# Lags that shrink one at a time over the last 24 groups of a graph-network kernel

## The chip, the cores and the metric

The kernel runs on one core of a Trainium2 chip. The metric is the device time of one execution in microseconds (us), lower is better. A core has five engines with a queue of instructions each, worked off in order: TensorE (PE in the profile; its weight loads are PEld), VectorE (DVE), ScalarE (ACT), GpSimd (POOL) and SyncE (SP). They wait for each other on semaphores. DMAs are issued from the queues of SyncE, ScalarE and GpSimd.

## The reference

There are 12,500 nodes with 64 features each, `x`, and 200,000 edges with a source, a target (sorted), 64 features and a distance. Cut to what matters:

```python
nodes = node_state[edges].reshape(num_edges, -1)          # source and target rows, 128 wide
gates = ssp(edge_state @ We1 + be1) @ We2 + be2           # ssp(x) = softplus(x) - log 2
soft_cutoff = 1.0 - sigmoid(5.0 * (edges_distance - 3.5))
gates = gates * soft_cutoff
h = ssp(nodes @ Wn1 + bn1) @ Wn2 + bn2
messages = h * gates
message_sum = zeros_like(node_state).at[edges[:, 1]].add(messages)
new_state = node_state + (ssp(message_sum @ Ws1 + bs1) @ Ws2 + bs2)
x = layernorm(x + new_state)
```

So every edge passes two small networks of two layers (one on its own features, one on its two nodes), the products are summed by target node, and then every node passes one more network of two layers and a normalization.

## The kernel before

**Groups.** Edges are worked in 391 groups of 512, numbered 0 to 390. A group is 4 lanes of 128 edges. Since targets are sorted, the targets of half a group lie in a window of 42 nodes; window positions are read from a table at run time.

**Stages of a group g**, with the line that the profile shows for each:
- `gather` (L230): GpSimd fetches the source rows, one indirect DMA per lane, into one of 18 buffers `xg`, 14 groups ahead. For 40 lanes out of the whole, SyncE and ScalarE fetch the 128 rows one by one instead (`fetch`, L244 loads row numbers into registers, L250 issues the DMAs): eight rows a step from ScalarE's queue, in three places of its step, six from SyncE's.
- `load` (L270, L278): SyncE fetches edge features `eT` and 42 rows per half group of a table with the target's share of layer 1, into `wns`, five steps ahead.
- `onehot` (L285): VectorE writes the edges' places in the window, 0 or 1, beside the source rows.
- `transposes` (L299, L296 for rows fetched one by one): TensorE, four, into a PSUM tile `tx` (two buffers); `xcopy` (L304): ScalarE copies it to SBUF.
- layer 1: `layer1_bias` (L309), `layer1_edge` (L314), `layer1_node` (L320): TensorE, into a PSUM tile `z` of two banks (two buffers).
- `exps` (L331), `logs` (L334): ScalarE; `softplus` (L339): VectorE, which makes `s`.
- layer 2: `layer2_edge` (L345 the biases, L348 the edges' half), `layer2_node` (L354): TensorE, into `gh` (two buffers).
- `hcut` (L363) and `message` (L367): VectorE.
- `scatter` (L371): TensorE sums messages by place in the window; `window` (L388): VectorE adds this to `sums` at the window's position.

**Node blocks.** Nodes are finished in blocks of 512 as soon as their sums are complete: `hidden` (L407) and `clamp` (L422, L423), logarithms (L426, L427), centring (L417, L418), `ssp` (L430), second layer (L435, L438) and `add` (L442), square, variance, root, scale (L446 to L464) and the store (L467). The parts of a block are dealt out to later steps. Parts with a TensorE half are called early in a step.

**Order.** All is written out by hand in program order (`manual_schedule`); each engine keeps that order, and waits are derived from the tiles. A program loop runs over steps i. In the main loop step i does, on TensorE: layer 1 bias of group i+1 (this instruction also takes, in one place, the waits for the loads and the copy of i+1 and for gather and one-hot of group i+3), layer 2 of edges of group i-1, layer 1 of i+1, sums of i-3 (into a free part of the `z` tile of i+1), transposes of i+3, layer 2 of nodes of i-1. So three lags exist: transposes are 2 groups ahead of layer 1, layer 2 is 2 groups behind it (`second`), sums are 4 behind it (`third`).

**Catch-up.** The last steps shrink these lags. `ends` is the step 10 before the last group (380). The lag of sums falls by one after step 378 and once more after 385, that of layer 2 after 383; from step 380 on, a second form of the step is used (the `else` branch): transposes and copy of the next group, layer 1, exponential and logarithm, layer 2 of group i, softplus of i+1, and then the sums, into a `tx` tile, with their window. Then a tail handles group 390, the last sums, and the last node block.

Of the kernel before, what the change touches and what calls it, by code (L numbers as in the profile page):

```python
# [59 lines left out]
HE = 256  # L60
GE = 2 * HE
W = 42
DW = D + W
PIECES = 3
NB = 512
K = 4
AHEAD = 14
LOADS = 5
SPREADS = 5
CATCH_UP = 10  # L70
PREPARE = 5
# [50 lines left out]
def gnn_resnorm_kernel(ctx: ExitStack, tc: tile.TileContext, a: dict, out: bass.AP, E: int):  # L122
    nc = tc.nc
# [64 lines left out]
    def note(key, ins):  # L188
        made.setdefault(key, []).append(ins)
        return ins  # L190
# [18 lines left out]
    def arrived(g, k):  # L209
        n = by_rows[g, k]  # L210
        queue = slots[n][0]
        n -= firsts[queue]
        return landed[queue][n % LANDED], 16 * P * (n // LANDED + 1)
# [77 lines left out]

    def transposes(g):
        tx = tx_tile()[:DW].rearrange("f (k e) -> f k e", k=K)
        for k in range(K):
            if (g, k) in by_rows:
                note(("rows read", by_rows[g, k]), nc.tensor.transpose(tx[:, k, :], xrs[g, k][:, :DW], ident)  # L296
                     .wait_op(*arrived(g, k), "sem-ge"))
            else:
                nc.tensor.transpose(tx[:, k, :], xgs[g][:, k, :DW], ident)  # L299
        xTs[g] = tx  # L300

    def xcopy(g):
        xT = work.tile([DW, K, P], F32, name="xT", bufs=3)
        note(("xcopy", g), nc.scalar.copy(xT, xTs[g]))  # L304
        xTs[g] = xT.rearrange("f (t h) e -> f h t e", h=2)
# [35 lines left out]

    def layer2_edge(g):
        gh = gh_tile()
        v = gh.rearrange("p (i t h d) -> p i t h d", i=2, t=2, h=2)
        nc.tensor.matmul(gh, ones3[:, :P], row3.rearrange("q i k d -> q (i k d)"), start=True, stop=False,  # L345
                         skip_group_check=True)
        for t in range(2):
            nc.tensor.matmul(v[:, 0, t], ss[g][:, 0, t, :], we2, start=False, stop=False, skip_group_check=True)  # L348
        ghs[g] = gh.rearrange("p (i k d) -> p i k d", i=2, k=K)

# [127 lines left out]
    with tc.manual_schedule():  # L478
# [130 lines left out]
        with tc.tile_pool(name="finish", bufs=1) as finish:  # L609
            blocks = list(zip(node_blocks(N), block_steps(N, NG)))  # L610
            last = NG - 1
            ends = last - CATCH_UP
            second, third, ahead = {}, {}, {}

            def lagging(i, lag, steps):

                lag -= sum(i > step for step in steps)
                return [g for g in range(i - lag, i - lag + 1 + (i in steps)) if g >= 0]

            for i in range(-3, NG):  # L620
                second[i] = lagging(i, 1, (ends + 3,))
                third[i] = lagging(i, 3, (ends - 2, ends + 5))
                ahead[i] = [i + 3] if i < ends else [i + 2] if i == ends + 1 else [i + 1] if i > ends + 2 else []
            parts, begun, complete, rest = {}, None, 0, []
# [9 lines left out]
            for i in range(-3, last - 1):  # L634
# [5 lines left out]
                if i >= 0:  # L640
                    at(gather, i + AHEAD, i < BEHIND)
                if i < ends:
                    needs = [("xcopy", i + 1), ("load", i + 1)]
                    needs += [(name, g) for g in ahead[i] for name in ("gather", "onehot")]
                    if i >= -1:
                        layer1_bias(i + 1, *needs)
                    for g in second[i]:
                        layer2_edge(g)
                    if i >= -1:
# [25 lines left out]
                else:  # L675
                    for g in ahead[i]:
                        transposes(g)
                        xcopy(g)
                    layer1_bias(i + 1)
                    layer1_edge(i + 1)  # L680
                    for part in early:
                        part.tensor(zs[i + 1][:, 1, HE:])
                    layer1_node(i + 1)
                    exps(i + 1)
                    logs(i + 1)
                    for g in second[i]:
                        layer2(g)
                        hcut(g)
                        message(g)
                    softplus(i + 1)  # L690
                    for g in third[i]:
                        scatter(g, tx_tile()[:, : 2 * W])
                        window(g)
                    for part in early:
# [19 lines left out]

            begun.pop(2).others()
            transposes(last)
            xcopy(last)
            layer1_bias(last)
            layer1_edge(last)
            layer1_node(last)  # L720
# [4 lines left out]
            square()  # L725
            for g in range(last - 2, last + 1):
                window_bases(g)
            layer2(last - 1)
            scatter(last - 2, tx_tile()[:, : 2 * W])
            softplus(last, edge)  # L730
            hcut(last - 1)
            message(last - 1)
            layer2_edge(last)
            scatter(last - 1, tx_tile()[:, : 2 * W])
            softplus(last, node)
            window(last - 2)
            variance()
            root()
            layer2_node(last)
            window(last - 1)  # L740
            hcut(last)
            message(last)
            scatter(last, tx_tile()[:, : 2 * W])
            window(last)
            hidden, clamp = begun.pop(0)
# [153 lines left out]
```

## Time and profile before

| | |
|---|---|
| time, median of 3 runs | 1969.16 us (1963.82 to 1975.15) |
| profiled execution: time, span | 1968.45 us, 1966.5 us |
| PE busy, mean granted clock | 1750.5 us (89%), 0.97 |
| GpSimd's last gather is issued | 1919.68 us |
| first exponential of group 366, of group 380, of group 390 | 1820.64, 1887.75, 1946.17 us |
| first layer of the last node block starts | 1952.89 us |

The profile is one execution. Busy time counts what an engine worked; matmuls are pipelined, so their rows overlap, and the distance between starts tells more than their length. In a timeline a row is start, length, engine, line, operation and shapes, the number of instructions merged, and in brackets the idle time ahead and what ended it. The granted clock is TensorE's clock as a share of full speed. Program line numbers are those of the kernel before.

### The profile page before, as it was taken

The numbers are of one execution on the slowest core, as the hardware profiler recorded it, in microseconds if no ns is written. First come the engines' busy times: TensorE is split into PE (matmuls) and PEld (weight loads), VectorE is DVE, ScalarE is ACT, GpSimd is POOL, SyncE is SP. The second block draws the span as 40 slices with busy tenths as digits, with TensorE's granted clock in tenths as the row PEclk, the third lists the DMA queues.
The fourth block names the chain that finished last, engine by engine and source line by source line (L and its number), as shares of the span: only waits on it lengthen the run. The fifth ranks groups of instructions, "written<-read, shape, count | busy, mean of one in ns | idle before, by whom it ended". The sixth has DMA issues, their size and how long they took to land.

```text
span 1966.5 us, 46634 instructions
## 1 busy us (share of the span) xinstructions
PE 1750.5 (89%) x11373; PEld 1491.4 (76%) x11373; DVE 1077.2 (55%) x2774; ACT 922.5 (47%) x1318; POOL 1445.0 (73%) x1527
## 2 busy tenths in 40 slices
PE   5899999999998988889889988998989989998896
PEld 4777877877777777777777777777777777777775
DVE  4455555555555555555555555555555555555654
ACT  1344545555454444445444444444544454444443
POOL 6777777777777777777777777777777777777770
PEclk9999999999999999999999999999999999999997
DMA  8422222222222222222222222222222222222220
GB/s 242 128 70 65 70 64 72 65 72 65 73 67 73 65 73 67 67 66 69 65 69 66 67 70 67 69 67 70 68 70 73 64 74 68 70 72 71 69 61 13
DMA packets 149240, 143.45 MB, mean 73 GB/s; under 512 B 50073, under 2 KB 96621, under 8 KB 148964
## 3 DMA queue, kind: packets, MB, share of 16 engines
q1 hardware_dynamic: 92972, 88.12, 15.6%
q0 software_dynamic: 48736, 50.00, 11.3%
q10 hardware_dynamic: 7256, 2.27, 0.6%
q8 instruction: 97, 1.59, 0.3%
q14 instruction: 179, 1.47, 0.3%
HBM read 130.59 MB, written 9.63 MB: 71 GB/s over the span
## 4 chain that ended last, share of the span: by engine, by line
PE 46%; ACTq 14%; DMA 10%; SPq 10%; issue 9%; ACT 5%; DVE 3%; POOL 3%; DVEq 0%; POOLq 0%
ACTq L250 11%; PE z L320 10%; PE gh L348 7%; PE gh L354 6%; PE z L314 5%; PE z L371 5%; DMA xg<-in_x,src_i 4%; PE tx L299 4%; DMA wns<-table 4%; SPq L250 4%; ACT u L331 3%; ACTq L244 3%; PE z L309 3%; POOL xg L230 3%; PE gh L345 2%
## 5 line engine op out<-in xcount | busy, mean ns | idle before, releaser
L230 POOL DMA_INDIRECT xg<-in_x,src_i x1523 | 1444.8, 949 | 475.3 <-issue 319.4
L331 ACT ACTIVATE u<-z 128x768 f32<-128x768 f32 x392 | 315.9, 806 | 624.4 <-PE z L371 316.7
L334 ACT ACTIVATE u<-u,one 128x768 f32<-128x768 f32 x392 | 366.0, 934 | 238.5 <-ACT u L331 236.7
L339 DVE SCALAR_TENSOR_TENSOR s<-u,z 128x768 f32<-128x768 f32 x392 | 372.6, 950 | 171.2 <-ACT u L334 154.6
L363 DVE TENSOR_TENSOR h<-gh,cut 128x256 f32<-128x256 f32 x391 | 165.2, 423 | 478.3 <-PE gh L354 472.0
L320 PE MATMUL z<-xT,wns 106*128 106x256 f32 x1564 | 423.9, 395 | 0.0
L354 PE MATMUL gh<-consts,s 128*128 128x64 f32 x3128 | 395.7, 270 | 0.0
L354 PEld LDWEIGHTS gh<-consts,s 128*128 128x128 f32 x3128 | 384.7, 194 | 0.0
L320 PEld LDWEIGHTS z<-xT,wns 106*128 106x128 f32 x1564 | 307.4, 198 | 45.8 <-ACT xT L304 0.7
L348 PEld LDWEIGHTS gh<-consts,s 128*128 128x128 f32 x1564 | 206.7, 192 | 122.8 <-issue 122.3
L348 PE MATMUL gh<-consts,s 128*128 128x128 f32 x1564 | 282.4, 304 | 0.0
L371 PEld LDWEIGHTS z<-xg,msg 128*128 128x128 f32 x1512 | 237.9, 199 | 22.9
L309 PE MATMUL z<-ones,be 3*128 3x256 bf16 x391 | 105.3, 269 | 167.8 <-DMA wns<-table 64.9
L299 PE MATMUL tx<-consts,xg 128*106 128x128 f32 x1524 | 240.8, 280 | 4.0 <-DVE xg L285 2.7
L388 DVE TENSOR_TENSOR sums<-sums,z 64x42 f32 x756 | 148.7, 197 | 171.4 <-ACT u L331 75.2
L314 PE MATMUL z<-eT,consts 128*128 128x256 f32 x782 | 242.4, 393 | 0.0
L304 ACT COPY xT<-tx 106x512 f32<-106x512 f32 x391 | 221.6, 567 | 15.5 <-PE tx L299 15.3
L371 PE MATMUL z<-xg,msg 128*128 128x84 f32 x1512 | 223.3, 271 | 0.0
L309 PEld LDWEIGHTS <-be 3*128 3x128 bf16 x391 | 35.4, 91 | 206.6 <-issue 102.9
L299 PEld LDWEIGHTS tx<-consts,xg 128*106 128x106 f32 x1524 | 181.8, 144 | 5.1 <-DVE xg L285 3.0
L367 DVE TENSOR_TENSOR msg<-gh,h 128x256 f32<-128x256 f32 x391 | 165.9, 424 | 13.4
L345 PE MATMUL gh<-row,ones 3*128 3x512 bf16 x391 | 145.9, 373 | 0.0
(103 smaller groups left out, 714.0 us busy)
## 6 DMA issues: line engine op xcount, KB each, us to landing
eT<-in_eT SPq DMA_DIRECT2D x195, 256.0 KB
xr<-in_x ACTq DMA_DIRECT2D x2944, 0.2 KB
xr<-in_x SPq DMA_DIRECT2D x2176, 0.2 KB
xg<-in_x,src_i POOLq DMA_INDIRECT x1523
wns<-table SPq DMA_DIRECT2D x782, 21.0 KB
table<-tb SPq DMA_DIRECT2D x14, 448.0 KB
sums<-in_xT SPq DMA_DIRECT2D x7, 455.0 KB
y<-in_x SPq DMA_DIRECT2D x24, 128.0 KB
```

Source lines behind the costliest of these rows:

```text
L230: note(("gather", g), nc.gpsimd.indirect_dma_start(out=xg[:, k, :D], out_offset=None, in_=x, in_offset=bass.IndirectOffsetOnAxis(ap=src_i[ ...
L250: ins = queues[queue].dma_start(row_tiles[n, "in"][r + j : r + j + 1, :D].bitcast(U8), x_bytes[:, bass.ds(row_at[queue][j], 4 * D)])
L299: nc.tensor.transpose(tx[:, k, :], xgs[g][:, k, :DW], ident)
L304: note(("xcopy", g), nc.scalar.copy(xT, xTs[g]))
L314: nc.tensor.matmul(zs[g][:, 0, :HE], we1.rearrange("a h d -> a (h d)"), eTs[g], start=False, stop=True, skip_group_check=True)
L320: nc.tensor.matmul(zn, wns[:, g % REST, h, :], xTs[g][:, h], start=True, stop=True, skip_group_check=True)
L331: nc.scalar.activation(us[g][:, part], z_of(g)[:, part], AF.Exp)
L334: nc.scalar.activation(us[g][:, part], us[g][:, part], AF.Ln, bias=one)
L339: nc.vector.scalar_tensor_tensor(ss[g].rearrange("p i t e -> p (i t e)")[:, part], us[g][:, part], BIG, z_of(g)[:, part], OP.min, OP.max)
L348: nc.tensor.matmul(v[:, 0, t], ss[g][:, 0, t, :], we2, start=False, stop=False, skip_group_check=True)
L354: nc.tensor.matmul(ghs[g][:, 1, 2 * t + h, :], ss[g][:, 1 + h, t, :], wn2, start=False, stop=h == 1 and t == 1, skip_group_check=True)
L371: ins = nc.tensor.matmul(sc, msgs[g][:, 2 * t : 2 * t + 2, :].rearrange("p h f -> p (h f)"), xgs[g][:, 2 * t : 2 * t + 2, D:DW], start=t = ...
```

## The change

The second form of the step gets another order and is used for 21 steps (368 to 388) in place of 9 (380 to 388). In it TensorE does transposes of group i+1, both biases, the sums (into the free part of the `z` tile, as in the main loop), layer 1 of i+1, and then all of layer 2 of its group. VectorE adds windows ahead of h and message, and softplus comes after them. Parts of node blocks go behind layer 2, into a `tx` tile. Transposes of this form wait at their first instruction for the loads, gather and one-hot of their group.

The lags shrink at one step each: transposes from 3 groups ahead to 1 in steps 366 and 367, which are main-loop steps that transpose nothing; layer 2 after step 374 (374 does two groups); sums after 376 and after 378. The biases of layer 2 are a function of their own, `layer2_bias`; in the main loop it is called where these biases stood before. The tail is put in the same order, with layer 2 of group 390 ahead of h and message of 389.

```diff
-CATCH_UP = 10
+CATCH_UP = (24, 16, 14, 12)
...
-    def transposes(g):
+    def transposes(g, *needs):
...
+            if k == 0:
+                behind(ins, *needs)
...
-    def layer2_edge(g):
+    def layer2_bias(g):
         gh = gh_tile()
-        v = gh.rearrange("p (i t h d) -> p i t h d", i=2, t=2, h=2)
         nc.tensor.matmul(gh, ones3[:, :P], row3.rearrange("q i k d -> q (i k d)"), start=True, stop=False,
                          skip_group_check=True)
+        ghs[g] = gh.rearrange("p (i k d) -> p i k d", i=2, k=K)
+
+    def layer2_edge(g):
+        v = ghs[g].rearrange("p i (t h) d -> p i t h d", t=2)
         for t in range(2):
             nc.tensor.matmul(v[:, 0, t], ss[g][:, 0, t, :], we2, start=False, stop=False, skip_group_check=True)
-        ghs[g] = gh.rearrange("p (i k d) -> p i k d", i=2, k=K)
...
-            ends = last - CATCH_UP
+            ends, *takes = (last - n for n in CATCH_UP)
...
-                second[i] = lagging(i, 1, (ends + 3,))
-                third[i] = lagging(i, 3, (ends - 2, ends + 5))
-                ahead[i] = [i + 3] if i < ends else [i + 2] if i == ends + 1 else [i + 1] if i > ends + 2 else []
+                second[i] = lagging(i, 1, takes[:1])
+                third[i] = lagging(i, 3, takes[1:])
+                ahead[i] = [i + 3] if i < ends else [i + 1] if i > ends + 1 else []
...
-                if i < ends:
+                if i < ends + 2:
...
                     for g in second[i]:
+                        layer2_bias(g)
                         layer2_edge(g)
...
                 else:
-                    for g in ahead[i]:
-                        transposes(g)
-                        xcopy(g)
+                    transposes(i + 1, ("load", i + 1), ("gather", i + 1), ("onehot", i + 1))
+                    xcopy(i + 1)
                     layer1_bias(i + 1)
+                    for g in second[i]:
+                        layer2_bias(g)
+                    for n, g in enumerate(third[i]):
+                        scatter(g, zs[i + 1][:, 1, HE + 2 * W * n : HE + 2 * W * (n + 1)])
                     layer1_edge(i + 1)
-                    for part in early:
-                        part.tensor(zs[i + 1][:, 1, HE:])
                     layer1_node(i + 1)
                     exps(i + 1)
                     logs(i + 1)
+                    for g in third[i]:
+                        window(g)
                     for g in second[i]:
                         layer2(g)
                         hcut(g)
                         message(g)
+                    for part in early:
+                        part.tensor(tx_tile())
                     softplus(i + 1)
-                    for g in third[i]:
-                        scatter(g, tx_tile()[:, : 2 * W])
-                        window(g)
                     for part in early:
                         part.others()
...
-            transposes(last)
+            transposes(last, ("load", last), ("gather", last), ("onehot", last))
             xcopy(last)
             layer1_bias(last)
+            layer2_bias(last - 1)
+            scatter(last - 2, zs[last][:, 1, HE : HE + 2 * W])
...
-            for g in range(last - 2, last + 1):
+            window(last - 2)
+            for g in range(last - 1, last + 1):
                 window_bases(g)
             layer2(last - 1)
-            scatter(last - 2, tx_tile()[:, : 2 * W])
+            layer2_bias(last)
             softplus(last, edge)
+            layer2_edge(last)
+            softplus(last, node)
+            layer2_node(last)
             hcut(last - 1)
             message(last - 1)
-            layer2_edge(last)
             scatter(last - 1, tx_tile()[:, : 2 * W])
-            softplus(last, node)
-            window(last - 2)
             variance()
             root()
-            layer2_node(last)
-            window(last - 1)
             hcut(last)
             message(last)
             scatter(last, tx_tile()[:, : 2 * W])
+            window(last - 1)
             window(last)
```

More of the change, by code (lines that the diff above doesn't have):

```diff
@@ L295, in transposes @@
             if (g, k) in by_rows:
-                note(("rows read", by_rows[g, k]), nc.tensor.transpose(tx[:, k, :], xrs[g, k][:, :DW], ident)
-                     .wait_op(*arrived(g, k), "sem-ge"))
-            else:
-                nc.tensor.transpose(tx[:, k, :], xgs[g][:, k, :DW], ident)
+                ins = nc.tensor.transpose(tx[:, k, :], xrs[g, k][:, :DW], ident)
+                note(("rows read", by_rows[g, k]), ins.wait_op(*arrived(g, k), "sem-ge"))
+            else:
+                ins = nc.tensor.transpose(tx[:, k, :], xgs[g][:, k, :DW], ident)
+            if k == 0:
+                behind(ins, *needs)
         xTs[g] = tx
```

## The prediction

> **What bounds the kernel now.** I read the page's busy shares and costliest groups, then GpSimd's own timeline, then the start of every exponential (line 331) as the clock of the steps, then TensorE's timeline in a step without waits and in the last steps, and last the busy time and granted clock in stretches of 3.4 us.
>
> ```profile
> PE 1750.5 (89%) x11373; PEld 1491.4 (76%) x11373; DVE 1077.2 (55%) x2774; ACT 922.5 (47%) x1318; POOL 1445.0 (73%) x1527
> ...
> L230 POOL DMA_INDIRECT xg<-in_x,src_i x1523 | 1444.8, 949 | 475.3 <-issue 319.4
> ```
>
> ```profile
> 1918.43 0.94 POOL L230 DMA_INDIRECT xg<-in_x,src_i  x1 [0.31 <-issue]
> 1919.68 0.95 POOL L230 DMA_INDIRECT xg<-in_x,src_i  x1 [0.30 <-issue]
> ```
>
> GpSimd looks 73% busy, but its gathers follow each other every 1.25 us (0.95 busy, 0.30 of issue) from the start to 1920.6: 4.99 us for a group of four gathers, 3.74 for one of three. That paces the main loop. A step without waits needs less of TensorE:
>
> ```profile
> 1884.87 0.28 PE L309 MATMUL z<-ones,be 3*128 3x256 bf16 x1
> 1884.99 0.37 PE L345 MATMUL gh<-row,ones 3*128 3x512 bf16 x1
> 1885.29 0.71 PE L348 MATMUL gh<-consts,s 128*128 128x128 f32 x4
> 1885.84 0.60 PE L314 MATMUL z<-eT,consts 128*128 128x256 f32 x2
> 1886.28 1.03 PE L320 MATMUL z<-xT,wns 106*128 106x256 f32 x4
> 1887.14 0.57 PE L371 MATMUL z<-xg,msg 128*128 128x84 f32 x4
> 1887.55 0.60 PE L299 MATMUL tx<-consts,xg 128*106 128x128 f32 x4
> 1887.98 1.00 PE L354 MATMUL gh<-consts,s 128*128 128x64 f32 x8
> 1888.92 0.28 PE L309 MATMUL z<-ones,be 3*128 3x256 bf16 x1
> ```
>
> From start to start that is 4.05 us: 0.12 first bias, 0.30 second bias, 0.55 layer 2 of edges, 0.44 layer 1 of edges, 0.86 layer 1 of nodes, 0.41 sums, 0.43 transposes, 0.94 layer 2 of nodes. Layer 1 of group i+1 waits, by its list of needs, for the gather of group i+3, so TensorE stays some two groups behind what it could do. The last gather is issued at 1919.68, yet group 390, the last, starts its exponential only at 1946.17 and the end is at 1966.5. The place to look at is this stretch:
>
> ```profile
> 1820.64 0.79 ACT L331 ACTIVATE u<-z 128x768 f32<-128x768 f32 x1
> ...
> 1920.49 0.94 DVE L339 SCALAR_TENSOR_TENSOR s<-u,z 128x768 f32<-128x768 f32 x1
> 1921.35 0.95 DVE L388 TENSOR_TENSOR sums<-sums,tx 64x42 f32 x4
> ...
> 1921.87 1.05 PE L299 MATMUL tx<-consts,xg 128*106 128x128 f32 x4 [1.31 <-issue]
> ...
> 1936.91 0.74 PE L438 MATMUL z<-consts,l_s 128*128 128x128 f32 x4 [2.01 <-DVE l_s L430]
> ...
> 1946.17 0.38 ACT L331 ACTIVATE u<-z 128x256 f32<-128x256 f32 x1 [2.39 <-PE z L320]
> ```
>
> The first line is the exponential of group 366, the last that of group 390: 125.5 us for 24 groups, 5.23 each. In its last ten steps the mean is 5.84. The lines between show two of the causes: transposes wait for a `tx` buffer that two sums hold until softplus and window are through, and the node block's second layer waits on TensorE for VectorE. And each such stall has an aftermath in the granted clock:
>
> ```profile
> 1863.90:1867.30 3.40, 1.61 (x10) 1.25 (x11) 2.93 (x9) 0.75 (x2) 2.49 (x4) 1.00 0.31 98
> 1867.30:1870.70 3.40, 3.40 (x15) 3.13 (x14) 0.56 (x2) 1.07 (x2) 2.57 (x3) 0.50 0.16 34
> 1918.50:1921.90 3.40, 2.09 (x20) 1.97 (x20) 2.04 (x6) 1.13 (x2) 1.82 (x2) 1.00 0.13 29
> 1921.90:1925.30 3.40, 3.40 (x10) 2.47 (x11) 1.03 (x4) 0.58 (x1) 0.00 (x0) 0.50 0.02 5
> ```
>
> The columns are the stretch, its length, busy time of PE, PEld, DVE, ACT, POOL, the granted clock, and DMA. A stretch in which TensorE was busy 1.6 to 2.3 of 3.4 us is followed by one at clock 0.50. Between 1820 and 1946 that is so at 1836.6, 1867.3, 1921.9 and (6.8 us long) 1939.0: five stretches, each worth up to 1.7 us, 8.5 together.
>
> **The change, part by part.** Up to the step of layer 1 of group 366 both kernels issue the same; the bias matmul split off layer 2 of edges stays at its place there. So I count from 1820.64 to the first exponential of group 390, and then the rest.
>
> *Two steps without transposes (groups 367, 368).* Transposes to 368 are already made. ScalarE bounds these: before, its round is 4.32 (exponential 0.81, half the row fetches 0.65, logarithm 0.94, four row DMAs 1.39, copy 0.57, overlaps off). 3.95 as before for 367, then 4.32 less a copy, 3.75: 1828.3. ScalarE's row fetches end with step 367 (736 pieces, two a step); SyncE's earlier. So none is dropped by the longer catch-up.
>
> *The turn (369).* The copy of 369 comes behind the logarithm of 368 (2.40 after its exponential) and behind the last four row DMAs (1.39), takes 0.57, and layer 1 of nodes to the exponential is 1.07 to 1.17 in this trace: 1833.8. Before had 1833.23; TensorE idles some 1.5 us once.
>
> *The new step.* Order: transposes, biases, sums, layer 1, layer 2. From the same rows: 0.53 (transposes to a bias, as in the old catch-up steps) + 0.12 + 0.31 + 0.43 + 0.44 + 0.86 + 0.55 + 0.84 = 4.08. What must hide: (a) the copy of `xT`. From transposes to layer 1 of nodes TensorE has 1.83 us of biases, sums and edges; the old catch-up step, which has less between, waits 1.27 there. Without cover it would cost nothing up to 1.27. (b) Layer 2 of a group now follows its own layer 1 by one step. From layer 1 of nodes: exponential at 1.07, logarithm to 2.85, softplus 0.94 behind h and msg on VectorE, to 4.3; layer 2 comes at 4.08 + 0.86 = 4.94. Slack 0.6; if VectorE is later by more, the excess is paid in every step. (c) Windows now stand ahead of h and msg on VectorE and read the bank that the exponential reads, so they wait for it (before already: VectorE's windows waited 75.2 us for line 331): 1.93 to 2.4 after layer 1, while h can start at 2.45. Free by a hair. (d) Transposes now wait at one place for the gather, loads and one-hot of their own group, and all of TensorE is queued behind them; from 1829 to 1928 these have landed some 4 to 8 us earlier (2.5 to 3.6 after the issues above), and SyncE's loads are issued five steps ahead still. Without that cover each microsecond late costs one.
>
> Ten steps (370 to 379) at 4.08: 40.8. In them one extra layer 2 with its bias (0.30 + 0.55 + 0.84), two extra sums (0.82) and one node block's two matmul parts (0.86 + 0.78): 4.2. Group 379 at 1878.8.
>
> *Sums lagging by one (380 to 390).* Here a chain closes: layer 2 to h 1.59 (1913.60 to 1915.18), h and msg 0.88, to the sums 0.12, then sums, edges, nodes 1.73 back to layer 2: 4.32, 0.24 above TensorE's own 4.08. Eleven steps: 47.5. Two node blocks, 3.3 less 4 x 0.24 that fills that gap: 2.3. Their second layer now stands behind layer 2, after its input is made, so the 2.01 stall goes, and sums no longer take a `tx` buffer, so the 1.31 goes. Group 390 at 1928.6. The period's bounds: 4.05, no gap at all, to 4.5, which the old catch-up step takes where it is undisturbed (1913.38 to 1917.89).
>
> *Clock.* With TensorE busy over 90% of each step, only the turn and a block step can lower it. Between none and the five of before (8.5 us) I take one and a half, 2.5 us, near the row that is all busy: 1931.1.
>
> [...]
>
> *The end.* From the exponential of 390 to the end is 20.3 before. The reordered tail takes VectorE's h and msg of 389 from between the two softplus halves, but queues them ahead of those of 390: I work out 0.35 less (6.7 to 6.35 up to the last node block's first layer). Half to one us either way is possible. The node block itself, 13.6, and its store stay.
>
> Sum: 1931.1 + 20.0 = 1951.1 of span, and 1.95 around it as now (1968.45 for 1966.5): 1953.0, 15.4 below the profiled time. That time lies 0.7 below the median 1969.16, so I say 1954.
>
> **Rivals.**
> *Gathers set the floor.* Last issue 1919.68; gathers landed 2.5 to 3.6 after issue (1857.03 to 1859.54, 1862.04 to 1865.68); 2.9 from transposes to the exponential: group 390 cannot start before 1925. With no gaps and full clock: 1947. For it: the rows above need no more. Against: the 4.32 chain, node blocks.
> *VectorE becomes the bound of the step.* With windows behind the exponential, and block work (scale and centring 2.0 us in one step) in the same queue, h and msg come late, and sums and layer 2 with them. Plus 0.5 in each of 21 steps gives 1964; the price at the old undisturbed 4.5 would be 1958. Against: from msg to the next h VectorE needs 1.7 us (softplus 0.95, one-hot 0.33, window 0.41) of 3.4 that it has.
> *Slower.* One mechanism: layer 2 waits in TensorE's queue for a softplus of the same step, TensorE's idle share passes about 30%, and the clock halves again and again. It decides at a wait of about 0.7 us a step (period 5.0 with the extras gives no gain); at the old catch-up's 5.84 in all 21 steps group 390 starts at 1956.4, and the time is 1978. Against: the slack in (b).
>
> **How the numbers follow.** The forecast has 0.62, the floor 0.08, VectorE's bound 0.18, slower 0.12. Half a per cent, about what a measurement of this kernel can tell from no change, is 9.8 us. So faster (below 1959.3) 0.70, within 0.18, slower 0.12. The range takes in the floor's edge and most of VectorE's case: 1946 to 1966. The forecast's own range is 1949 to 1959.
>
> **What would show it.** Right: steps of 4.1, then 4.3 us between exponentials from group 370 on, the first exponential of 390 near 1931, three or fewer half-clock stretches after 1820, no TensorE idle over 0.3 us ahead of transposes or line 353 (layer 2 of edges), and GpSimd ending at 1920.6 as before. Wrong: TensorE waiting for VectorE ahead of the sums or layer 2 in each step, half-clock stretches inside the new steps, or gathers that end later because buffers come free later.

## The result, and the profile after

| | before | after |
|---|---|---|
| time, median of 20 runs each | 1969.88 us (1962.87 to 1979.13) | 1962.85 us (1955.84 to 1975.31) |
| ratio after / before | | 0.9958, 95% interval 0.9944 to 0.9971 |
| profiled execution: time, span | 1968.45, 1966.5 us | 1957.03, 1955.1 us |
| first exponential of 366, of 390 | 1820.64, 1946.17 us | 1820.72, 1934.44 us |

By the ratio the change makes the kernel faster by 0.42%, about 8 us; the two medians lie 7.0 us apart. The forecast was 1954 us and 15 us of gain: the sign and the range (1946 to 1966) held, the forecast's own narrower range (1949 to 1959) did not, and half of the gain is missing. The profiled execution gains 11.4 us, and it is the third shortest of the twenty; both gaps are taken up below.

The busy shares and the gathers of the page, kernel after (columns as before):

```profile
PE 1735.4 (89%) x11373; PEld 1480.4 (76%) x11373; DVE 1077.7 (55%) x2774; ACT 923.3 (47%) x1318; POOL 1445.7 (74%) x1527
...
L230 POOL DMA_INDIRECT xg<-in_x,src_i x1523 | 1445.5, 949 | 475.5 <-issue 328.2
```

TensorE's busy time fell from 1750.5 to 1735.4 us with the same 11373 matmuls: they did not become fewer, more of them ran at the full clock. Not all of that is the change. Up to group 366, where both kernels issue the same, TensorE is busy for 1625.63 us before and 1619.01 after, so 6.6 of the 15.1 us are a difference between two executions; 8.2 lie in the catch-up (116.11 and 107.91). GpSimd's work is unchanged. Line numbers have moved: the exponential is L333, the logarithm L336, the copy of `xT` L306, layer 1 L311, L316 and L322, layer 2 L346, L353 and L358, h L367, msg L371, sums L375, windows L392, softplus L341, the node block's first layer L411. One of the new steps, from TensorE's timeline of the kernel after, then the last gather on GpSimd's and the first exponential of group 390 on ScalarE's:

```profile
1908.08 0.60 PE L299 MATMUL tx<-consts,xg 128*106 128x128 f32 x4
1908.61 0.28 PE L311 MATMUL z<-ones,be 3*128 3x256 bf16 x1
1908.73 0.37 PE L346 MATMUL gh<-row,ones 3*128 3x512 bf16 x1
1909.22 0.68 PE L375 MATMUL z<-xg,msg 128*128 128x84 f32 x4
1909.73 0.63 PE L316 MATMUL z<-eT,consts 128*128 128x256 f32 x2
1910.20 1.03 PE L322 MATMUL z<-xT,wns 106*128 106x256 f32 x4
1911.07 0.61 PE L353 MATMUL gh<-consts,s 128*128 128x128 f32 x4
...
1920.48 0.94 POOL L230 DMA_INDIRECT xg<-in_x,src_i  x1 [0.30 <-issue]
1934.44 0.38 ACT L333 ACTIVATE u<-z 128x256 f32<-128x256 f32 x1 [1.97 <-PE z L322]
```

No row of TensorE has an idle time in brackets. The last gather is issued at 1920.48 (1919.68 before), so group 390 starts its exponential 14.0 us after it, where it was 26.5.

Where the time went, by the exponentials as marks (us; the last two columns use the first row of the node block's first layer):

| kernel | 366 to 371 | 371 to 390 | 390 to the block's first layer | from there to the end | sum |
|---|---|---|---|---|---|
| before | 22.96 | 102.57 | 6.72 | 13.61 | 145.86 |
| after, profiled execution | 24.22 | 89.50 | 7.81 | 12.85 | 134.38 |

The new steps gain 13.07 us; the stretch around the turn (where the new form takes over from the main loop) loses 1.26 and the approach to the last node block 1.09. The block itself gains 0.76, which the two further runs below do not repeat.

Busy time and granted clock in stretches (columns as in the prediction), first the 24 groups as a whole, then around the turn:

```profile
1820.70:1934.40 113.70, 107.91 (x707) 89.11 (x708) 70.95 (x192) 58.70 (x87) 76.33 (x81) 0.98 0.25 58
1830.80:1834.20 3.40, 0.27 (x2) 0.27 (x2) 1.14 (x2) 1.21 (x2) 2.49 (x4) 1.00 0.41 100
1834.20:1837.60 3.40, 3.40 (x14) 3.05 (x14) 0.39 (x2) 1.71 (x3) 2.57 (x3) 0.50 0.20 42
```

The mean clock over the catch-up is 0.98; for 1820.6 to 1946.2 of the kernel before the same view gives 0.93. From 1820 to the exponential of 390 one half-clock stretch is left of five, and it lies at the turn. (In both kernels the clock also falls to half in the tail, at 1952.6 before and 1940.0 after, and stays there to the end.) That turn, group 369, in ScalarE's and TensorE's timelines of the kernel after:

```profile
1830.49 0.94 ACT L336 ACTIVATE u<-u,one 128x768 f32<-128x768 f32 x1 [0.69 <-ACT u L333]
1830.57 2.69 ACTq L250 DMA_DIRECT2D xr<-in_x  x6
1833.30 0.58 ACT L306 COPY xT<-tx 106x512 f32<-106x512 f32 x1 [1.87 <-issue]
...
1830.17 0.63 PE L316 MATMUL z<-eT,consts 128*128 128x256 f32 x2
1833.94 1.88 PE L322 MATMUL z<-xT,wns 106*128 106x256 f32 x4 [3.13 <-ACT xT L306]
```

ACTq is ScalarE's instruction queue. The copy of `xT` 369 stands behind six row DMAs, which take 2.69 us; it starts at 1833.30, and TensorE idles 3.13 us ahead of layer 1 of the nodes. The forecast counted only the last four of the six, 1.39 us, behind the end of the logarithm. The stretch with TensorE busy for 0.27 of 3.40 us is followed by one at clock 0.50.

### The profile page after: what moved, and what is told of

Same layout as the page of the kernel before. It is cut to its first block, busy times and chain, and to the rows that moved or that the text cites. A ratio compares the mean times of both kernels' runs of the same rounds, so it can differ in the third digit from the quotient of the medians.

```text
span 1955.1 us, 46668 instructions
## 1 busy us (share of the span) xinstructions
PE 1735.4 (89%) x11373; PEld 1480.4 (76%) x11373; DVE 1077.7 (55%) x2774; ACT 923.3 (47%) x1318; POOL 1445.7 (74%) x1527
## 3 DMA queue, kind: packets, MB, share of 16 engines
q14 instruction: 179, 1.47, 0.3%
## 4 chain that ended last, share of the span: by engine, by line
PE 43%; ACTq 20%; DMA 10%; issue 9%; ACT 6%; SPq 6%; DVE 4%; POOL 2%; DVEq 0%; POOLq 0%
ACTq L250 16%; PE z L322 10%; PE gh L353 6%; PE gh L358 6%; PE z L316 5%; PE z L375 5%; ACT u L333 4%; ACTq L244 4%; DMA xg<-in_x,src_i 4%; DMA wns<-table 4%; PE tx L299 3%; PE z L311 2%; SPq L250 2%; PE gh L346 2%; POOL xg L230 2%
## 5 line engine op out<-in xcount | busy, mean ns | idle before, releaser
L333 ACT ACTIVATE u<-z 128x768 f32<-128x768 f32 x392 | 316.0, 806 | 616.1 <-PE z L375 284.9
L336 ACT ACTIVATE u<-u,one 128x768 f32<-128x768 f32 x392 | 366.0, 934 | 237.6 <-ACT u L333 233.8
L341 DVE SCALAR_TENSOR_TENSOR s<-u,z 128x768 f32<-128x768 f32 x392 | 372.7, 951 | 177.4 <-ACT u L336 168.1
L322 PE MATMUL z<-xT,wns 106*128 106x256 f32 x1564 | 419.9, 392 | 3.1 <-ACT xT L306 3.1
L367 DVE TENSOR_TENSOR h<-gh,cut 128x256 f32<-128x256 f32 x391 | 165.5, 423 | 425.5 <-PE gh L358 418.9
L358 PE MATMUL gh<-consts,s 128*128 128x64 f32 x3128 | 393.7, 269 | 0.0
L358 PEld LDWEIGHTS gh<-consts,s 128*128 128x128 f32 x3128 | 382.0, 193 | 0.1
L322 PEld LDWEIGHTS z<-xT,wns 106*128 106x128 f32 x1564 | 305.5, 197 | 48.7 <-ACT xT L306 3.9
L353 PEld LDWEIGHTS gh<-consts,s 128*128 128x128 f32 x1564 | 208.7, 192 | 119.7 <-issue 116.4
L353 PE MATMUL gh<-consts,s 128*128 128x128 f32 x1564 | 280.0, 302 | 1.7 <-DVE s L341 1.7
L392 DVE TENSOR_TENSOR sums<-sums,z 64x42 f32 x778 | 153.0, 197 | 207.1 <-ACT u L333 117.2
L375 PEld LDWEIGHTS z<-xg,msg 128*128 128x128 f32 x1556 | 240.1, 196 | 30.9 <-DVE msg L371 4.8
L311 PE MATMUL z<-ones,be 3*128 3x256 bf16 x391 | 105.2, 269 | 169.8 <-DMA wns<-table 53.8
L316 PE MATMUL z<-eT,consts 128*128 128x256 f32 x782 | 241.1, 391 | 0.0
L375 PE MATMUL z<-xg,msg 128*128 128x84 f32 x1556 | 229.9, 271 | 2.1 <-DVE msg L371 1.5
L306 ACT COPY xT<-tx 106x512 f32<-106x512 f32 x391 | 221.7, 567 | 12.5 <-PE tx L299 10.0
L311 PEld LDWEIGHTS <-be 3*128 3x128 bf16 x391 | 35.4, 91 | 210.2 <-issue 110.7
L371 DVE TENSOR_TENSOR msg<-gh,h 128x256 f32<-128x256 f32 x391 | 166.0, 425 | 13.4
L346 PE MATMUL gh<-row,ones 3*128 3x512 bf16 x391 | 145.9, 373 | 0.1
```

The costliest lines, as they stand in the source:

```text
L316: nc.tensor.matmul(zs[g][:, 0, :HE], we1.rearrange("a h d -> a (h d)"), eTs[g], start=False, stop=True, skip_group_check=True)
L322: nc.tensor.matmul(zn, wns[:, g % REST, h, :], xTs[g][:, h], start=True, stop=True, skip_group_check=True)
L333: nc.scalar.activation(us[g][:, part], z_of(g)[:, part], AF.Exp)
L336: nc.scalar.activation(us[g][:, part], us[g][:, part], AF.Ln, bias=one)
L341: nc.vector.scalar_tensor_tensor(ss[g].rearrange("p i t e -> p (i t e)")[:, part], us[g][:, part], BIG, z_of(g)[:, part], OP.min, OP.max)
L358: nc.tensor.matmul(ghs[g][:, 1, 2 * t + h, :], ss[g][:, 1 + h, t, :], wn2, start=False, stop=h == 1 and t == 1, skip_group_check=True)
```

## The experiments

**The changed kernel again.** Two further runs of the same kernel tell which parts of its trace are fixed.

> The changed kernel once more, as the yardstick for the runs beside it: 0.994 to 0.997 of before. Its profile tells whether the profiled execution of the result (1957.03) was a quick one: the first exponential of 390 near 1934 and 1.0 us of window and register loads ahead of the tail's first softplus should show again; what makes other executions 6 us longer should show in the start of the exponential of 366 (gathers) or after it (steps).

> The changed kernel once more, beside the next two on one chip. Theory (the turn at group 369 sets the scatter): ratio 0.994 to 0.997; in its trace group 371 to group 390 takes 89.5 us as in the two traces of it so far, and what differs between its executions is the time from the exponential of 366 to that of 371 (24.2 and 27.6 so far) and the phase of the gathers. Rival (the scatter lies in the new steps): 371 to 390 differs from 89.5 by over 0.5.

Measured: 1961.81 us, ratio 0.9946 (0.9924 to 0.9968), and 1961.37 us, ratio 0.9952 (0.9934 to 0.9969). In all three traces 371 to 390 takes 89.50 us, and 390 to the block's first layer 7.81. What differs is 366 to 371 (24.22, 27.55, 24.22) and the time at which group 366 starts (1820.72, 1822.73, 1822.20). The long one has three half-clock stretches at the turn, from the same view of that run:

```profile
1832.40:1835.80 3.40, 1.70 (x10) 0.85 (x8) 2.33 (x6) 1.03 (x2) 2.48 (x4) 0.99 0.30 61
1835.80:1839.20 3.40, 2.86 (x10) 2.50 (x10) 0.00 (x0) 1.24 (x2) 2.48 (x4) 0.50 0.28 80
1839.20:1842.60 3.40, 3.40 (x16) 2.43 (x15) 2.05 (x6) 1.89 (x4) 2.59 (x3) 0.50 0.19 35
1842.60:1846.00 3.40, 3.40 (x11) 2.86 (x12) 0.30 (x2) 0.00 (x0) 2.68 (x3) 0.50 0.17 29
```

The end differs too: from the block's first layer on it takes 12.85, 13.71 and 13.77 us. So in these three traces the scatter of this kernel lies in the turn, in what comes before 366 and in the last node block, not in the new steps. The profile that the forecast can be held against is a good draw: its span is 2.4 and 6.2 us shorter than the other two. TensorE's idle time at the turn is 3.13, 2.25 and 3.16 us in the three, and three half-clock stretches follow the shortest of them, one each of the others: the length of the gap alone does not set the price.

**The turn one group later.** After step 367 ScalarE fetches no rows.

```diff
-CATCH_UP = (24, 16, 14, 12)
+CATCH_UP = (23, 16, 14, 12)
```

> The first number of the catch-up is 23 in place of 24, so the first copy of the new step no longer stands behind ScalarE's last row DMAs. Theory (the turn costs 3.7 us: 3.1 of TensorE idle and a half-clock stretch after it, both behind six row DMAs and a register load on ScalarE): no TensorE idle over 0.3 us at the turn, no half-clock stretch there, the exponential of 390 starts 3 to 4 us earlier than in the changed kernel, time 0.15 to 0.2% below it. Rival (what is lost at the turn is made up later, because gathers, loads or VectorE set the pace after it): the stall goes, the exponential of 390 starts within 1 us of the changed kernel's.

Measured: 1958.73 us, ratio 0.9926 (0.9900 to 0.9952), beside 0.9946 (0.9924 to 0.9968) for the changed kernel on the same chip; the two intervals overlap. ScalarE's and TensorE's timelines of this run at the turn, now group 370:

```profile
1833.75 2.71 ACTq L250 DMA_DIRECT2D xr<-in_x  x6
1836.56 0.81 ACT L333 ACTIVATE u<-z 128x768 f32<-128x768 f32 x1 [1.95 <-DVE h L367]
1837.40 0.93 ACT L336 ACTIVATE u<-u,one 128x768 f32<-128x768 f32 x1
1838.24 0.40 ACT L450 ACTIVATE y<-y 128x256 f32<-128x256 f32 x1
1838.55 0.56 ACT L306 COPY xT<-tx 106x512 f32<-106x512 f32 x1
...
1839.16 1.13 PE L322 MATMUL z<-xT,wns 106*128 106x256 f32 x4 [1.39 <-ACT xT L306]
```

No row DMA stands between the logarithm and the copy any more. TensorE idles 1.39 us, no half-clock stretch follows, and 366 to 371 takes 20.52 us instead of 24.22 and 27.55. The expectation of no idle over 0.3 us failed. The same six row DMAs now stand ahead of the exponential of 369, which starts right behind them, 2.0 us after layer 1 of its group has ended (1833.52 + 1.03), and the copy of 370 comes in the queue behind it; that what is left of the idle comes from there is read from these rows and was not tried with a turn one group later still.

So the row DMAs right ahead of the copy cost about 1 to 2 us of idle time. What follows in half-clock stretches is not settled by one run: the last version below has the same turn, idles 1.62 us and pays three. Nor does all of the gain reach the end here: this execution had its half-clock stretch later, at 1885.7, behind the wait for msg in step 379 that is told under the windows, so 380 came 6.45 after 379 instead of 5.19, and 371 to 390 took 90.81. From 366 to 390 it is 2.4 and 5.7 us shorter than in the traces above.

**The new form of the step, started late; the old form, started early.** Is it the form or the length of the catch-up? One run gives the changed kernel the old length, the other gives the kernel before a long one.

```diff
-CATCH_UP = (24, 16, 14, 12)
+CATCH_UP = (10, 7, 5, 3)
```

> The new step, but with the catch-up over the last 10 groups as before (10, 7, 5, 3). Theory (the gain is the form of the step: no stalls on tx buffers and node blocks, hence no half clock): 4.1 to 4.4 us a step from 382 on in place of 5.84, the exponential of 390 at 1936 to 1939, 0.9955 to 0.997 of before, most of the gain. Rival (the gain is the early start, which frees TensorE from waiting for gathers two groups ahead): 0.999 or more of before.

```diff
-CATCH_UP = 10
+CATCH_UP = 22
```

> The old step, with its catch-up over 22 groups in place of 10 (24 would leave out row fetches). Theory (form of the step): 4.5 us in undisturbed steps, 6 to 8 in steps with a node block or two sums, three or more half-clock stretches after 1830; the exponential of 390 at 1945 to 1950, 0.998 to 1.003 of before. Rival (early start): 0.997 of before or less.

Measured: the new form started late 1962.53 us, ratio 0.9953 (0.9935 to 0.9971), the same gain as the whole change; from 381 to 390 it takes 43.62 us where before takes 53.45 and the changed kernel 41.39. That is 4.85 a step, more than the 4.1 to 4.4 expected, since the steps in which the lags shrink are among them. The old form started early 1973.99 us, ratio 1.0020 (0.9998 to 1.0042): no gain at all. Its undisturbed steps are 4.50, but steps with a part of a node block or with two sums take 5.3 to 6.4, and the last three 7.9 to 8.2. Stretches from 1926 on in the run of the old form:

```profile
1926.10:1929.50 3.40, 1.99 (x13) 1.17 (x12) 3.02 (x8) 1.21 (x3) 0.00 (x0) 1.00 0.27 77
1929.50:1932.90 3.40, 3.40 (x11) 2.13 (x11) 0.00 (x0) 0.84 (x2) 0.00 (x0) 0.51 0.00 0
1932.90:1936.30 3.40, 3.40 (x18) 3.40 (x18) 0.95 (x3) 0.90 (x1) 0.00 (x0) 0.50 0.00 0
1936.40:1939.80 3.40, 3.40 (x10) 2.14 (x8) 1.62 (x5) 0.59 (x1) 0.00 (x0) 0.50 0.00 0
```

One stretch with 1.4 us of TensorE idle, a wait for the node block's `l_s` ahead of its second layer, and the clock stays at half to the end of the execution. So without the new form there is no gain, and with it the late start gains as much as the early one. That the early start is worth nothing is not shown: from the exponential of 366 to that of 390 the late start takes 116.48 us, the three traces of the changed kernel 113.72, 117.05 and 113.72, and the run with the turn at 370 takes 111.33. The new steps save time early too, and the turn takes it back; 1958.73 us with the turn at 370 against 1962.53 here points the same way, though the intervals overlap. The forecast had not separated form and start.

**Windows behind softplus.** In the new step VectorE adds windows before h and msg.

```diff
-                    for g in third[i]:
-                        window(g)
                     for g in second[i]:
                         layer2(g)
                         hcut(g)
                         message(g)
                     for part in early:
                         part.tensor(tx_tile())
                     softplus(i + 1)
+                    for g in third[i]:
+                        window(g)
```

> In the new step the windows go behind softplus, out of the way of h and message. Theory (windows cost only where two groups are added in one step, which showed as 1.0 us of TensorE idle ahead of the sums of 380; elsewhere the chain layer 2, h, message, sums sets 4.3): from the exponential of 371 to that of 390 1.0 to 1.4 us less than the 89.5 of the changed kernel, undisturbed steps stay at 4.27 to 4.32. Rival (VectorE is the bound of the step, windows waiting for the exponential hold h back in every step): 3 us less or more, undisturbed steps at 4.1.

This run, and the next two, fell on a chip on which the kernel before takes 2462.39 us: its main loop needs some 6.0 us a group there, so only steps late in the catch-up compare with the rest. Ratio 0.9971 (0.9945 to 0.9997), on that chip. From 381 to 390 it took 40.73 us, 41.39 in the changed kernel. I ran the same kernel again on a chip with the usual times:

> The edit of e4_window_last alone: windows behind softplus on VectorE. On the slower chip of that run, groups 381 to 390 took 40.7 against 41.4. Theory (windows delay h and msg where two sums or a block step fill VectorE): 371 to 390 falls from 89.5 to 87.5 to 88.8, ratio 0.993 to 0.996. Rival (windows are free): 89.5 +- 0.3, the time that of the changed kernel.

Measured: 1959.34 us, ratio 0.9937 (0.9917 to 0.9956), beside 0.9952 (0.9934 to 0.9969) for the changed kernel on that chip: the two intervals overlap, so the times alone don't decide. The steps do: 371 to 390 falls from 89.50 to 87.50 us. 380 takes 4.27 instead of 5.19, and 374, 381 and 387, which carry a node block's first layer, 5.01 instead of 5.34; that is 1.9 of the 2.0, and the last version below takes the same 4.27 and 5.01. (The rest of this execution took longer: three half-clock stretches at the turn, where 366 to 371 took 27.23, and a clock that fell to half 3.9 us after the exponential of 390 and not 5.5 us, with 8.67 us to the block's first layer.) The step before group 380 in VectorE's and TensorE's timelines of the kernel after:

```profile
1883.36 0.43 DVE L392 TENSOR_TENSOR sums<-sums,z 64x42 f32 x2 [2.10 <-ACT u L333]
1884.27 0.42 DVE L392 TENSOR_TENSOR sums<-sums,z 64x42 f32 x2 [0.48 <-DVE sums L392]
1884.72 0.42 DVE L367 TENSOR_TENSOR h<-gh,cut 128x256 f32<-128x256 f32 x1
1885.18 0.42 DVE L371 TENSOR_TENSOR msg<-gh,h 128x256 f32<-128x256 f32 x1
...
1885.66 0.68 PE L375 MATMUL z<-xg,msg 128*128 128x84 f32 x4 [1.03 <-DVE msg L371]
```

VectorE waits 2.10 us for the exponential, because the windows read its bank, then adds two windows with 0.48 between them; h starts late, and TensorE idles 1.03 us for msg. In an ordinary step there is one window, and h could not have started sooner: layer 2 ends just then. There 4.27 stays 4.27.

**The tail.** Softplus of the nodes and its layer 2 ahead of the last windows, so that h and msg of 390 come sooner.

```diff
             square()
-            window(last - 2)
-            for g in range(last - 1, last + 1):
-                window_bases(g)
             layer2(last - 1)
             layer2_bias(last)
             softplus(last, edge)
             layer2_edge(last)
-            softplus(last, node)
-            layer2_node(last)
             hcut(last - 1)
             message(last - 1)
+            softplus(last, node)
+            layer2_node(last)
+            for g in range(last - 2, last + 1):
+                window_bases(g)
+            window(last - 2)
             scatter(last - 1, tx_tile()[:, : 2 * W])
```

> The changed kernel with h and message of 389 again between the softplus halves, and the window of 388 and the register loads for the last windows behind them. Theory (the new tail loses about 1.4 us because window and register loads stand ahead of the first softplus half): from the first exponential of 390 to the last block's first layer 6.0 to 6.7 us in place of 7.81. Rival (the last group's own chain sets this, whatever VectorE does first): 7.4 or more.

> All three together: 23 in place of 24, windows behind softplus, the mended tail. Theory: the gains add, 3.7 at the turn (more where the clock stays low longer), 1.2 and 1.3: 6 us or more below the changed kernel, 0.990 to 0.993 of before, the exponential of 390 near 1930. Rival (gathers set the floor from here on): TensorE waits for gathers ahead of transposes, and the time is that of the run with 23 alone, 0.9926.

The second is all three edits together. Measured, on the slower chip: 0.9992 (0.9966 to 1.0019) and 0.9966 (0.9939 to 0.9993). From the exponential of 390 to the block's first layer it took 7.84 and 7.82 us: the tail edit brought nothing, where 6.0 to 6.7 had been expected; and all three together missed their 0.990 to 0.993. VectorE's timeline of the run with all three shows why:

```profile
2427.26 0.68 DVE L341 SCALAR_TENSOR_TENSOR s<-u,z 128x512 f32<-128x512 f32 x1
2428.86 0.41 DVE L392 TENSOR_TENSOR sums<-sums,z 64x42 f32 x2 [0.93 <-issue]
2429.30 0.42 DVE L454 TENSOR_REDUCE var<-y 128x4 f32<-128x256 f32 x1
2429.75 0.42 DVE L367 TENSOR_TENSOR h<-gh,cut 128x256 f32<-128x256 f32 x1
```

The 0.93 us of issue are the register loads with the window positions. The edit had only moved them from ahead of softplus to ahead of h of 390, which starts 5.06 us after the exponential, as in the changed kernel (5.05).

**All three, with the register loads moved into a wait.** The loads now stand where VectorE waits for ScalarE anyway (1.47 us in the rows below).

```diff
-CATCH_UP = (24, 16, 14, 12)
+CATCH_UP = (23, 16, 14, 12)
...
             square()
+            for g in range(last - 2, last + 1):
+                window_bases(g)
             layer2(last - 1)
             layer2_bias(last)
             softplus(last, edge)
             layer2_edge(last)
             hcut(last - 1)
             message(last - 1)
             softplus(last, node)
             layer2_node(last)
-            for g in range(last - 2, last + 1):
-                window_bases(g)
             window(last - 2)
```

(The second part is against the run before; windows stay behind softplus.)

> Three mends in one: the turn one group later, windows behind softplus, and in the tail the register loads of the last windows ahead of the first softplus half, with softplus of the nodes and its layer 2 ahead of the window. Theory: the shortfall of the forecast lies in these three. Turn 3 to 6 us less from 366 to 371, steps 1 less, and from the exponential of 390 to the node block's first layer 7.2 instead of 7.8; a time of 1955 to 1959 where before is 1970, ratio 0.9915 to 0.9945. Rival (the gathers' phase decides the end anyway): no shorter than the changed kernel by 2 us in the median, though its steps are.

Measured: 1953.30 us (1951.94 to 1956.26), ratio 0.9910 (0.9892 to 0.9927). On the same chip the changed kernel took 1957.70 to 1965.59 in its runs: no overlap. This version beats both, and it comes out below its own expectation of 1955 to 1959. VectorE's timeline of its tail:

```profile
1935.16 0.42 DVE L341 SCALAR_TENSOR_TENSOR s<-u,z 128x256 f32<-128x256 f32 x1 [1.47 <-ACT u L333]
...
1936.29 0.68 DVE L341 SCALAR_TENSOR_TENSOR s<-u,z 128x512 f32<-128x512 f32 x1
1936.89 0.40 DVE L392 TENSOR_TENSOR sums<-sums,z 64x42 f32 x2
...
1938.17 0.42 DVE L367 TENSOR_TENSOR h<-gh,cut 128x256 f32<-128x256 f32 x1 [0.43 <-PE gh L358]
```

h of 390 starts 4.46 us after its exponential at 1933.71 and waits only for layer 2; the block's first layer comes after 7.21 us, not 7.81. 371 to 390 takes 87.38 us. At the turn this execution was costly: TensorE idled 1.62 us there and three half-clock stretches followed, so 366 to 371 took 25.11, where the other run with the turn at 370 had 20.52. Its profiled execution took 1956.13 us, nearly the longest of its six.

The gains of the single edits, 3 us for the turn and 2 for the windows in the medians, 0.6 for the tail by its trace, add up to 5.7; the difference of the medians is 8.1. With six or seven runs a kernel, whose times spread by 4 to 10 us, this agrees, but the shares of the three are not settled to better than 2 or 3 us.

## Why the prediction was right, and where it was off

**The bound and the mechanism: right, with two causes of stalls not named.** TensorE's stalls and the half clock after them made the last groups slow. The 1.31 ahead of transposes and the 2.01 ahead of the block's second layer are gone, GpSimd's end moved by only 0.8 us, and no transposes wait for a gather. The run with the old form started early shows that without the new order nothing is gained. But the two stalls that the prediction names precede only three of the five half-clock stretches (1921.9, and 1939.0 with two). The other two, at 1836.6 and 1867.3, follow waits of layer 1's bias for loads, 1.10 us for `eT` and this one for `wns` in the kernel before:

```profile
1865.68 0.26 PE L309 MATMUL z<-ones,be 3*128 3x256 bf16 x1 [2.04 <-DMA wns<-table]
```

In the kernel after, TensorE waits for no load between 1821 and 1934; the run with the new form started late still has such a wait, 2.35 us at 1847.06, and two half-clock stretches behind it. This part of the gain came without having been reckoned.

**The two steps without transposes: 0.7 too little.** 368 was put at 1828.3 and came at 1828.99. Its round stayed 4.32 although the copy was gone: I took the copy's 0.57 off a sum of overlapping terms, but the row DMAs in ScalarE's queue set that round. From the first of the six behind the logarithm's start to the end of the last it is 2.68 us, with the copy among them (1826.13 to 1828.81 before) and without it (1826.21 to 1828.89 after).

**The turn: the step that failed.** Forecast 1833.8 with 1.5 us of idle, measured 1835.86 with 3.13; relative to 368, 1.4 us more than forecast. Half a microsecond of that is the copy: it starts 4.31 us after the exponential of 368 and not 2.40 + 1.39 = 3.79, since six row DMAs and not four stand ahead of it. Some 0.8 us is the clock: from the first row of layer 1 of nodes to the exponential it takes 1.92, counted as 1.07 to 1.17. The next step ran in part at half clock as well, 4.99 instead of 4.08. The 1.5 us of idle were too few even by the prediction's own terms: by them the copy ends 4.36 us after the exponential of 368, and TensorE ran out of work 1.82 us after it, which leaves 2.5. So the 1.39 us in the run with the turn one group later match the 1.5 only as a number. What I missed is the queue that the copy was moved behind.

**The new steps.** 371 to 373 take 4.09 each (forecast 4.08), steps with sums lagging by one 4.27 and 4.32 (4.32): right. The groups 370 to 379 took 46.66 us for 45.0, of which 0.91 is the half clock just told, and 380 to 390 took 51.92 for 49.8. Point (c), windows "free by a hair", holds for a step with one window and fails where two windows or a node block's part stand with them: 2.0 us in these 19 groups. "VectorE becomes the bound" thus came true in four steps of 21, and not at 0.5 in each. Point (b) held: from 1841 to 1934 the waits of TensorE's matmuls name msg twice, 1.5 us together, and softplus never.

**The clock.** I allowed 2.5 us for one and a half stretches and counted them beside the steps; the one that came is already in the steps, 0.8 us at the turn and 0.9 in the 4.99. So the sum to 390 is 1931.1 + 0.7 + 1.4 + 0.9 + 0.7 + 2.1 - 2.5 = 1934.4, as measured. The allowance was 0.8 us too high, by luck, and hid as much of what the row DMAs and the windows cost.

**The tail.** Forecast 0.35 less than before up to the block's first layer, measured 1.09 more. In the kernel after, VectorE waits 1.89 us for the exponential's second half before the window, then 0.99 for register loads, and only then comes the first softplus:

```profile
1935.88 0.41 DVE L392 TENSOR_TENSOR sums<-sums,z 64x42 f32 x2 [1.89 <-ACT u L333]
1937.27 1.02 DVE L341 SCALAR_TENSOR_TENSOR s<-u,z 128x256 f32<-128x256 f32 x2 [0.99 <-issue]
1937.75 0.71 PE L353 MATMUL gh<-consts,s 128*128 128x128 f32 x4 [1.74 <-DVE s L341]
```

In the kernel before no window stood there, and the register loads fell into VectorE's wait for the exponential:

```profile
1947.61 0.42 DVE L339 SCALAR_TENSOR_TENSOR s<-u,z 128x256 f32<-128x256 f32 x1 [2.87 <-ACT u L331]
```

I had counted the change of place of h and msg, but not the window that the new tail puts ahead of softplus, nor that the register loads behind it no longer fall into a wait. The block itself and its store took 0.76 less this time, so the whole tail is 20.66 us against 20.0.

**From the profile to the median.** The profiled execution ended at 1957.03, 4 us later than the 1953.0 worked out for it: the 3.3 to group 390 and 0.7 behind it. The median lies 5.8 us above the profiled execution, and that I could not have had from the steps. Which parts make it up in the other nineteen executions is not on record. The traces show what varies: the turn's half clock, one stretch in this trace and three in another, the start of 366, which lay between 1820.6 and 1823.9, and the last block, 0.9 us. I moved one execution's sum to a median by the distance that held for the kernel before (0.7 us).

**The chances.** "Faster by over 0.5%" got 0.70; 0.42% lies just on the other side, within 0.5%. That the range held is in part luck: 1962.85 lies in the part of it that was taken in for VectorE as the bound of every step, and what filled it was the turn, the tail, a few steps and the way from one execution to the median. The version with all three mends reaches 1953.3, the time of the forecast, though its trace still has 1.62 us of idle and three half-clock stretches at the turn; that the two numbers meet is no proof of the forecast's sum.

**The clock rule.** The Trainium skill's page "TensorE: Matmul & The Clock Gate", section "Why this matters for your kernels", asks for no idle gap over about 3 us. At the turn of the changed kernel the gap is 3.13, and rule and trace agree. But 1.62 us of idle in the last run and a stretch busy for 1.99 of 3.40 in the old form brought half clock too, and 1.39 in the run with the turn at 370 did not at once. The clock's changes in these traces come 3.41 us apart or a multiple of that. Cut at these points between 150 and 1946 us, the nine traces with the usual times show: after a full-clock stretch with TensorE busy for less than 1.9 us the clock always fell to half (39 of 39), after one with 2.7 us or more never (0 of 3613), and in between it fell 193 times in 810. So the busy share of such a stretch tells more than the length of one gap, and the prediction's "busy 1.6 to 2.3" does not always bring half clock. Whether a gap of 1.3 to 1.6 us costs anything depends on how it falls into these stretches.

## What to carry to other kernels

When a step is given a new order, walk each engine's queue through the first step in which the new order meets the old one, DMA issues and register loads included: the steady steps came out to 0.05 us here, and most of what was missed in the profiled execution lay at the seams (the turn, the tail, steps with one more window). A TensorE stall of 1.5 to 3 us is priced with the half-clock stretches that may follow, mostly one to three of them here, and their number differs from execution to execution, so one profile can't be carried to the median.

## What was not expected of the hardware

- After a stretch of 3.41 us with TensorE busy less than 1.9 us (56%) the clock was 0.50 in the next one in every case, from 1.9 to 2.7 us (79%) in one of four. How long it stays differs: at the turn one stretch in the kernel after, three in its second run and in the last version; in the run of the old form started early from 1929.5 to the end, although TensorE shows as busy for the whole of each of the seven stretches up to 1953.4. No run here tells why.
- Six row DMAs in ScalarE's queue keep it for 2.69 us, and the loads of window positions leave VectorE idle for 0.99 us (two groups, kernel after) and 0.93 us (three groups, run with all three edits), though the profile counts neither as busy.
- One chip ran the kernel before 25% slower (2462.39 us) and the three edited ones about as slowly, with TensorE's mean clock at 0.86 to 0.87 in their traces; the late steps of the catch-up took the same 4.27 and 4.97 us there. What slows its main loop is not shown.
